# Layer 2 of a four-layer model: where the routing of its experts is issued, and how its streams are woven together

## The chip, the core and the metric

The kernel runs on one NeuronCore of a Trainium2 chip. Five engines work side by side, each through its own queue of instructions: TensorE (PE: matmuls and transposes, results to PSUM), VectorE (DVE), ScalarE (ACT), GpSimd (POOL) and SyncE (SP, which here only issues DMAs). The metric is the device time of one execution, in microseconds. The granted clock in the profile is TensorE's, as a share of full speed.

## The reference

Four layers work on 2048 tokens of width 256, four sequences of 512. Each layer takes the normalised tokens and adds a mixer and a feed-forward block. Only layer 2 and the end of layer 1 matter here. Layer 2:

```python
# mixer: 16 heads of 16; key and value are one head of 16
q = (x @ Wq.T + bq).reshape(b, l, h, hd)
kv = (x @ Wkv.T + bkv).reshape(b, l, 2, hd)
k, v = (kv[:, :, 0], kv[:, :, 1])
attn = softmax(einsum('blhd,bld->blh', q, k)[..., None] / sqrt(hd), axis=-1)
out = (attn * v[:, :, None, :]).reshape(b, l, -1)
# experts: the 2 best of 8 by a softmax router, and a shared expert of width 256
scores = softmax(einsum('th,eh->te', xf, gate_w), axis=-1)
topk_w, topk_i = top_k(scores, 2)
topk_w = topk_w / sum(topk_w, axis=-1, keepdims=True)
hgated = silu(einsum('th,ehi->eti', xf, wg)) * einsum('th,ehi->eti', xf, wu)
y = ...   # the two chosen experts' hgated @ wd, weighted by topk_w
shared = silu(xf @ sg) * (xf @ su) @ sd
```

The reference's softmax in the mixer is over an axis of length one, so that its weight is 1 whatever the score; the kernel computes it in full. Layer 1 is a latent attention with causal softmax beside product-key experts and a gated feed-forward block.

## The kernel before

The tokens lie in SBUF as 16 tiles of 128 (`c.x`), with their normalised transpose in `c.xnT`. A layer is a set of Python generators, its streams, each of which issues some instructions and then yields a cost. `weave` (L230 and on) always advances the stream whose progress, cost so far over its stated total, is least; a third number is the progress at which a stream joins. Thus the weave sets the order in which instructions are issued in the program. The framework's scheduler then fixes each engine's own order from the priority of issue, its own estimates of durations and the dependences, places the tiles and inserts the semaphores; where the text marks `keep_in_program_order`, an instruction may not be moved against its like. On the chip every engine's queue runs in the order so found, and an instruction that waits holds up all that stand behind it.

When all users of a sequence in a layer have added their part (`part_done`), the layer norm of that sequence is issued (L91 to L126): statistics and `xn` on DVE, a store of the rows to DRAM, and, some steps later or when `settle` asks for it, the transposes into `xnT`.

Layer 2 treats the tokens in two halves of 1024. A half's routing, `dispatch`, takes the router's matmuls for 8 tiles (L142 on `t_small`), a softmax on DVE and ACT, the rank of each of the 8 experts by comparison of all pairs, counts by three small matmuls (L1303), and from these a slot for every chosen token, such that each expert's tokens fill whole tiles: 23 tiles of 128 slots hold any outcome. To invert that (which token stands in slot s?), 16 masks `at` of 128x128 are made (L1353) and multiplied by `hit` (L1360), which yields `ids`. Then `gather` (L1396) fetches the tokens' rows by 23 indirect DMAs from POOL's queue; `experts` transposes them (L1414), multiplies by the slot tile's expert (L1426, at a column offset that PE reads from memory), applies SiLU (L1433, L1434), transposes again (L1440), multiplies (L1448), copies (L1453) and stores the result (L1455) to DRAM. `combine` later fetches for each token tile the two results by indirect DMAs (L1492) and adds them, weighted, to `c.x` (L152).

The shared expert is a `glu_pieces` (L134 up, L201, L202, L212 down, L158 adds to x). The mixer, `head_mix`, works sequence by sequence: projections (L142 on `h_small`) and bias (L1184), product with the key (L1189), sum (L1193), Exp (L1198), normalisation (L1199, L1200), then the product with the value on POOL (L1201) and the addition to x on DVE (L1206).

Layer 1's weave ends with `room`, which at progress 0.915 closes the pools of the product-key and feed-forward streams and opens layer 2's first tiles (`following.first()`), and does no more. Layer 2's `run` then has three weaves, one after another: the shared expert beside both halves' routing; the first half's experts beside the mixer and the second half's gathers; the second half's experts beside the first half's combine. The first half's gathers are issued pair by pair from within `experts`, three pairs of buffers ahead. The second half's combine runs inside layer 3.

## Time and profile before

| | us |
|---|---|
| runs shown: median (lowest, highest) | 3180.86 (3175.3, 3186.27) |
| the profiled execution | 3176.93 |
| its span, first to last instruction | 3175.2 |
| layer 1's last matmul for its output (L882) ends | 1537.4 |
| first `ids` (L1366) of half 0, half 1 | 1559.2, 1598.7 |
| first and last row gather (L1396) | 1560.1, 1651.5 |
| first and last expert matmul of L1426 | 1609.8, 1710.1 |
| POOL's four products (L1201) | 1632.9 to 1675.9 |

A line of the profile names the engine, the line of the code (of a helper, where one records the operation), the operation, the tile written and those read, and shapes. A line of the timeline gives the start, the time that a run of equal instructions took, their number, and in brackets how long the engine had stood idle and who ended it. A line of the groups gives the number, busy time and mean, and the idle time before them. A line of the stretches gives the length, then PE, its weight loads, DVE, ACT and POOL each with busy time and number of instructions, and last the granted clock, DMA share and GB/s. Each float32 matmul shows as two instructions. A line of the waits gives who waited for whom, the sum, the number of waits, and the longest.

### The profile page before, as it was taken

The page shows a single profiled execution, that of the slowest core. Times are in us where ns is not written, and L with a number is a line of the kernel's source. Part 1 is how long each engine was busy: PE and PEld are TensorE (multiplying, and loading weights), DVE is VectorE, ACT ScalarE, POOL GpSimd, SP SyncE. Part 2 cuts the span into 40 slices and gives each one's busy share as a digit, 9 for nine tenths or more (in the row PEclk, how much of TensorE's full clock was granted, in tenths as well). Part 3 has the DMA queues.
Part 4 walks back from the last instruction along what each step waited for, and adds up shares of the span by engine and source line. Part 5 has one row for each costly group of instructions (what it writes and reads, how often), then busy time and mean ns, then how long its engine had stood idle before and what let it go on. Part 6 is the DMA issues. An engine that isn't in the chain of part 4 may idle for free.

```text
span 3175.2 us, 35804 instructions
## 1 busy us (share of the span) xinstructions
PE 3091.7 (97%) x12502; PEld 1890.4 (60%) x12502; DVE 1847.0 (58%) x4714; ACT 1259.5 (40%) x2910; POOL 636.4 (20%) x525
## 2 busy tenths in 40 slices
PE   8999999999899999999889999999999999999999
PEld 5566566565655555555566566566666665555555
DVE  5878778787677787777546654554554522222222
ACT  4444444443356666667425433333333401111111
POOL 0464455555400132331153000000000000000000
PEclk9999999999899999999889999999999999999999
DMA  3233233332311244444143000000000000000000
GB/s 130 83 104 123 87 97 111 102 108 75 107 37 35 62 123 102 114 110 132 38 107 110 7 21 7 1 27 1 21 1 1 20 20 20 20 20 20 1 0 27
DMA packets 89092, 185.16 MB, mean 58 GB/s; under 512 B 14193, under 2 KB 57217, under 8 KB 84177
## 3 DMA queue, kind: packets, MB, share of 16 engines
q1 hardware_dynamic: 74448, 135.05, 13.2%
q0 software_dynamic: 14176, 47.01, 6.0%
q8 instruction: 99, 1.62, 0.2%
q10 hardware_dynamic: 288, 0.82, 0.1%
q14 instruction: 81, 0.66, 0.1%
HBM read 160.95 MB, written 12.98 MB: 55 GB/s over the span
## 4 chain that ended last, share of the span: by engine, by line
PE 80%; DVE 10%; DMA 4%; ACT 2%; POOL 2%; issue 1%; SPq 1%; DVEq 0%; ACTq 0%; POOLq 0%
PE mm L134 31%; PE acc L212 8%; PE mm L643 7%; PE mm L142 5%; PE acc L1115 4%; PE acc L659 3%; DMA G<-own 3%; PE tr L1107 2%; PE tr L507 2%; DVE G L421 2%; PE tr L824 2%; PE acc L868 2%; DVE cy L280 2%; PE acc L486 1%; PE tr L212 1%
## 5 line engine op out<-in xcount | busy, mean ns | idle before, releaser
L134 PE MATMUL mm<-xnT,wu 128*128 128x512 f32 x2128 | 960.3, 598 | 2.9 <-DVE cy L280 1.3
L134 PEld LDWEIGHTS mm<-xnT,wu 128*128 128x128 f32 x2128 | 400.4, 191 | 464.5 <-issue 434.9
L650 ACT ACTIVATE pr<-pr,nm 128x128 f32<-128x128 f32 (+3 forms) x512 | 285.9, 559 | 293.5 <-DVE nm L646 290.9
L201 ACT ACTIVATE sg<-mm 128x512 f32<-128x512 f32 x176 | 104.5, 594 | 611.2 <-PE mm L134 611.1
L202 DVE TENSOR_TENSOR hT<-sg,mm 128x512 f32<-128x512 f32 x176 | 120.5, 685 | 385.8 <-PE mm L134 369.8
L646 DVE CUSTOM_DVE_ANT_0 pr<-mm,late 128x128 f32<-128x128 f32 (+3 forms) x512 | 245.2, 482 | 85.2 <-PE mm L643 80.3
L212 PE MATMUL acc<-wu,hT 128*128 128x256 f32 x1280 | 289.5, 382 | 1.9 <-DVE hT L202 1.4
L212 PEld LDWEIGHTS acc<-wu,hT 128*128 128x128 f32 x1280 | 243.2, 191 | 53.1 <-issue 18.0
L134 PE MATMUL mm<-xnT,w_in 128*128 128x512 f32 x512 | 230.9, 597 | 0.0
L986 POOL DMA_INDIRECT e<-in_p_experts,ids x128 | 128.1, 1001 | 453.6 <-DVE x L152 413.3
L421 DVE TENSOR_TENSOR_SCAN G<-G,eye 128x1024 f32<-128x1024 f32 x64 | 158.3, 2474 | 66.9 <-DMA G<-own 66.8
L447 POOL TENSOR_TENSOR G<-G,CB 128x1024 f32<-128x1024 f32 x64 | 151.9, 2374 | 176.4 <-DVE G L421 97.1
L643 PE MATMUL mm<-kf,qf 128*128 128x128 f32 (+3 forms) x512 | 176.2, 443 | 6.5 <-DVE qf L801 4.1
L643 PE MATMUL mm<-k,q 128*128 128x128 f32 (+3 forms) x512 | 176.6, 435 | 1.1 <-DVE q L1080 1.1
L280 DVE SCALAR_TENSOR_TENSOR cy<-mm,ws,cy 128x511 f32<-128x511 f32 (+2 forms) x216 | 158.4, 741 | 32.6 <-ACT cy L276 29.2
L134 PEld LDWEIGHTS mm<-xnT,w_in 128*128 128x128 f32 x512 | 97.6, 192 | 103.4 <-issue 97.8
L433 ACT ACTIVATE xD<-xc,ws 128x128 f32<-128x128 f32 x256 | 84.2, 391 | 176.8 <-POOL y L470 162.0
L152 DVE SCALAR_TENSOR_TENSOR x<-acc,cw,x 128x256 f32<-128x256 f32 x128 | 62.0, 484 | 155.6 <-PE acc L212 155.6
L1115 PE MATMUL acc<-PT,V 128*128 128x512 f32 (+3 forms) x512 | 149.5, 433 | 0.0
L1080 DVE TENSOR_SCALAR q<-mm,bias 128x512 f32<-128x512 f32 x64 | 48.0, 751 | 169.0 <-PE mm L134 169.0
L824 PEld LDWEIGHTS tr<-con,pr 128*128 128x128 f32 x640 | 80.5, 142 | 95.6 <-ACT pr L817 30.5
L507 PE MATMUL tr<-wo,y 128*128 128x256 f32 x512 | 126.7, 391 | 7.9 <-DVE x L158 4.0
(309 smaller groups left out, 4948.3 us busy)
## 6 DMA issues: line engine op xcount, KB each, us to landing
G<-own SPq DMA_DIRECT2D x64, 512.0 KB, 4.3
w_in<-in_m_units SPq DMA_DIRECT2D x16, 1024.0 KB, 5.1
eb<-since SPq DMA_DIRECT2D x96, 128.0 KB, 3.4
wu<-in_o_units SPq DMA_DIRECT2D x8, 1536.0 KB, 6.5
wo<-in_m_units SPq DMA_DIRECT2D x16, 512.0 KB, 4.1
psw<-pes SPq DMA_DIRECT2D x128, 64.0 KB, 2.8
wu<-in_g_units SPq DMA_DIRECT2D x4, 1536.0 KB, 6.9
wu<-in_f_units SPq DMA_DIRECT2D x4, 1536.0 KB, 8.2
```

The source lines that it names most:

```text
L134: c.nc.tensor.matmul(out, lhsT=w[:, d, cols], rhs=c.xnT[:, d, tokens], start=(d == 0), stop=(d == 1))
L142: c.nc.tensor.matmul(out, lhsT=c.xnT[:, d, tokens], rhs=w[:, d, cols], start=(d == 0), stop=(d == 1))
L212: nc.tensor.matmul(po[:, j, :], lhsT=hT[k][:, (t + j) * P : (t + j + 1) * P], rhs=wd[:, k, :], start=(i == 0), stop=(i == per - 1),)
L280: nc.vector.scalar_tensor_tensor(y[:, j:], src[:, : SEQ - j], conv[:, k, 3 - j : 4 - j], y[:, j:], ALU.mult, ALU.add,)
L421: nc.vector.tensor_tensor_scan(flat, flat, eye.rearrange("p h t -> p (h t)"), 0.0, ALU.mult, ALU.add)
L447: nc.gpsimd.tensor_mul(G, G, seqs[b][2][:, t, :][:, None, :].to_broadcast([P, HG, P]))
L507: nc.tensor.matmul(po, lhsT=y[:, k, :], rhs=groups[i][1][:, k, :], start=(k == 0), stop=(k == 3))
L643: nc.tensor.matmul(sc, lhsT=q[:, i * P : n], rhs=k[:, :n], start=True, stop=True)
L646: nc.vector.tensor_tensor_reduce(out=pr, in0=sc, in1=late[:, SEQ - n :], scale=1.0, scalar=-NEG, op0=ALU.add, op1=ALU.min, accum_out=nm,)
L650: nc.scalar.activation(pr, pr, AF.Exp, bias=nm, scale=-1.0, accum_out=total)
L824: nc.tensor.transpose(pt[:, (i - j) * P : (i - j + 1) * P], prs[s][i][:, j * P : (j + 1) * P], c.ident)
L1115: nc.tensor.matmul(z[:, j * P :], lhsT=head["V"][:, j, h, :], rhs=head["PT"][:, j, j * P :], start=(j == 0), stop=(j == TPB - 1),)
```

## The change

`room` in layer 1 goes on with the first half's routing after opening the tiles, and is given a total of 270 in place of 1, so that its 21 units of cost take it from 0.915 to about 0.99 of the weave. The two first weaves of layer 2 become one: the shared expert, the first half's gathers (a stream of its own), the second half's routing followed by its gathers, the first half's experts, and the mixer. The third weave stays; the combine joins at 0.15 in place of 0.2. Gathered rows have one ring of 20 pair buffers in place of 3 and 12.

In the routing, a router call serves both sequences of a half at once; the running sum over 8 tiles takes three doubling steps in place of eight single ones; the tile number (`token`) is multiplied into `hit` once, and the 16 masks are made by four wide comparisons in place of sixteen narrow ones, in the ring of buffers (`before`, 4) that the router's comparisons use; all matmuls of L1360 follow the masks in one run. The mixer takes two sequences at a time, with one Exp for both, a yield after it, and the second product on DVE in place of POOL, which keeps only DMAs. Layer 3's router uses the same function with one sequence a call.

```diff
@@ -1043,13 +1043,14 @@
             right.close()
             following.first()
             yield 1.0
+            yield from following.routing(0)
 
         weave(
             c,
             (latent, 457.0, 0.0),
             (product_key_pieces(c, a, p_keep, p_t, dram, xn), 232.0, 0.0),
             (glu_units(), 145.0, 0.0),
-            (room(), 1.0, 0.915),
+            (room(), 270.0, 0.915),
             flush=False,
         )
 
@@ -1169,43 +1170,51 @@
 
 
 
-def head_mix(c, pool, w, b):
+def head_mix(c, pool, w, bs):
 
     nc = c.nc
     H, HD, W = 16, 16, 288
     wqkv = v3(w[:, : 2 * W], W)
     bias = w[:, 2 * W : 3 * W]
-    qkv = c.tile(pool, [P, TPB, W], "qkv")
-    c.settle(b)
-    for t in range(TPB):
-        tt = b * TPB + t
-        pq = c.ps()[:, :W]
-        project_tokens(c, pq, wqkv, slice(0, W), slice(tt * P, (tt + 1) * P))
-        nc.vector.tensor_add(qkv[:, t, :], pq, bias)
-        yield 0.5
+    n = len(bs) * TPB
     full = [P, TPB, H, HD]
-    prod = c.tile(pool, full, "prod")
     heads = lambda v: v.rearrange("p t (h d) -> p t h d", d=HD)
-    nc.vector.tensor_mul(
-        prod, heads(qkv[:, :, :256]), qkv[:, :, 256:272][:, :, None, :].to_broadcast(full)
-    )
-    s = c.tile(pool, [P, TPB, H], "s", bufs=2)
-    nc.vector.tensor_reduce(s, prod, AX.X, ALU.add)
-    top = c.tile(pool, [P, TPB, H], "top", bufs=2)
+    qkv = c.tile(pool, [P, n, W], "qkv")
+    s = c.tile(pool, [P, n, H], "s")
+    parts = [slice(i * TPB, (i + 1) * TPB) for i in range(len(bs))]
+    for b, part in zip(bs, parts):
+        c.settle(b)
+        for t in range(TPB):
+            tt = b * TPB + t
+            pq = c.ps()[:, :W]
+            project_tokens(c, pq, wqkv, slice(0, W), slice(tt * P, (tt + 1) * P))
+            nc.vector.tensor_add(qkv[:, part.start + t, :], pq, bias)
+            yield 0.5
+        prod = c.tile(pool, full, "prod")
+        nc.vector.tensor_mul(
+            prod, heads(qkv[:, part, :256]),
+            qkv[:, part, 256:272][:, :, None, :].to_broadcast(full),
+        )
+        nc.vector.tensor_reduce(s[:, part], prod, AX.X, ALU.add)
+    top = c.tile(pool, [P, n, H], "top")
     nc.vector.tensor_copy(top, s)
     nc.vector.tensor_sub(s, s, top)
     nc.scalar.activation(s, s, AF.Exp, scale=HD ** -0.5)
+    yield 1.0
     nc.vector.reciprocal(top, s)
     nc.vector.tensor_mul(s, s, top)
-    nc.gpsimd.tensor_mul(
-        prod, s[:, :, :, None].to_broadcast(full),
-        qkv[:, :, 272:288][:, :, None, :].to_broadcast(full),
-    )
-    x = c.x[:, b * TPB : (b + 1) * TPB, :]
-    nc.vector.tensor_add(x, x, prod.rearrange("p t h d -> p t (h d)"))
-    c.part_done(b)
-    yield 1.0
+    for b, part in zip(bs, parts):
+        prod = c.tile(pool, full, "prod")
+        nc.vector.tensor_mul(
+            prod, s[:, part, :, None].to_broadcast(full),
+            qkv[:, part, 272:288][:, :, None, :].to_broadcast(full),
+        )
+        x = c.x[:, b * TPB : (b + 1) * TPB, :]
+        nc.vector.tensor_add(x, x, prod.rearrange("p t h d -> p t (h d)"))
+        c.part_done(b)
+        yield 0.5
 
 
 def softmax(c, s, m, scale):
@@ -1220,28 +1229,31 @@
     nc.vector.tensor_mul(s, s, m[:, :, None].to_broadcast(wide))
 
 
-def router(c, pool, wr, b, p=None):
+def router(c, pool, wr, bs, p=None, wide=1):
 
 
     nc = c.nc
-    E = 8
-    c.settle(b)
-    pl = c.ps()[:, : TPB * E]
-    for t in range(TPB):
-        tt = b * TPB + t
-        project_tokens(
-            c, pl[:, t * E : (t + 1) * E], wr, slice(0, E), slice(tt * P, (tt + 1) * P)
-        )
-    yield 0.5
+    E, n = 8, len(bs) * TPB
+    pl = c.ps()[:, : n * E]
+    for i, b in enumerate(bs):
+        c.settle(b)
+        for t in range(TPB):
+            tt, to = b * TPB + t, (i * TPB + t) * E
+            project_tokens(
+                c, pl[:, to : to + E], wr, slice(0, E), slice(tt * P, (tt + 1) * P)
+            )
+    yield 2.0
     if p is None:
         p = c.tile(pool, [P, TPB, E], "p")
     nc.vector.tensor_copy(p, v3(pl, E))
-    m = c.tile(pool, [P, TPB], "m")
+    m = c.tile(pool, [P, n], "m")
     softmax(c, p, m, 1.0)
-    full = [P, TPB, E, E]
+    yield 2.0
+    full = [P, n, E, E]
     other, own = p[:, :, None, :].to_broadcast(full), p[:, :, :, None].to_broadcast(full)
-    before = c.tile(pool, full, "before")
-    tie = c.tile(pool, full, "tie")
+    before = c.tile(pool, full, "before", bufs=wide)
+    tie = c.tile(pool, full, "before" if wide > 1 else "tie", bufs=wide)
     nc.vector.tensor_tensor(before, other, own, ALU.is_gt)
     nc.vector.tensor_tensor(tie, other, own, ALU.is_equal)
     low = v3(c.low, E)[:, None, :, :].to_broadcast(full)
@@ -1274,30 +1286,34 @@
         c, k, pool, nc = self.c, self.k, self.pool, self.c.nc
         tile = lambda shape, tag, **kw: c.tile(pool, shape, tag, **kw)
         p, rank = tile([P, HT, E8], "p_half"), tile([P, HT, E8], "rank")
-        for i in range(2):
-            tiles = slice(i * TPB, (i + 1) * TPB)
-            before = yield from router(c, pool, k["router"], 2 * self.hf + i, p[:, tiles, :])
-            nc.vector.tensor_reduce(rank[:, tiles, :], before[2], AX.X, ALU.add)
-            yield 1.0
+        before = yield from router(c, pool, k["router"], [2 * self.hf, 2 * self.hf + 1], p, 4)
+        yield 2.0
+        nc.vector.tensor_reduce(rank, before[2], AX.X, ALU.add)
 
         both = [P, 2, HT, E8]
         sel = tile(both, "sel")
         for r in range(2):
             nc.vector.tensor_scalar(sel[:, r], rank, float(r), None, ALU.is_equal)
-        chosen = tile([P, HT, E8], "chosen")
+        Z = 4
+        cum = tile([P, 4, Z + HT, E8], "cum")
+        nc.vector.memset(cum[:, :, :Z, :], 0.0)
+        chosen = cum[:, 0, Z:, :]
         nc.vector.tensor_scalar(chosen, rank, 2.0, None, ALU.is_lt)
-        cum = tile([P, HT + 1, E8], "cum")
-        nc.vector.memset(cum[:, 0, :], 0.0)
-        for t in range(HT):
-            nc.vector.tensor_add(cum[:, t + 1, :], cum[:, t, :], chosen[:, t, :])
-        yield 1.0
+        for step in range(3):
+            last, back = cum[:, step], 1 << step
+            nc.vector.tensor_add(
+                cum[:, step + 1, Z:, :], last[:, Z:, :], last[:, Z - back : Z - back + HT, :]
+            )
+        before_tile, in_all = cum[:, 3, Z - 1 : Z - 1 + HT, :], cum[:, 3, Z + HT - 1, :]
+        yield 3.0
         flat = lambda v: v.rearrange("p t e -> p (t e)")
         pc = c.ps()
         n = HT * E8
         for out, lhsT, rhs, start, stop in (
             (pc[:, :n], c.le, flat(chosen), True, False),
-            (pc[:, :n], c.ones, flat(cum[:, :HT, :]), False, True),
-            (pc[:, n : n + E8], c.ones, cum[:, HT, :], True, True),
+            (pc[:, :n], c.ones, flat(before_tile), False, True),
+            (pc[:, n : n + E8], c.ones, in_all, True, True),
         ):
             c.tc.keep_in_program_order(
                 nc.tensor.matmul(out, lhsT=lhsT, rhs=rhs, start=start, stop=stop)
@@ -1344,25 +1360,29 @@
             k["iota"][:, :NS][:, None, :].to_broadcast(by_tile), ALU.is_equal,
         )
         nc.vector.scalar_tensor_tensor(part, part, -float(P), slot, ALU.mult, ALU.add)
+        split = hit.rearrange("p (r t) j -> p r t j", r=2)
+        nc.vector.tensor_mul(
+            split, split, k["token"][:, None, :, None].to_broadcast([P, 2, HT, NS])
+        )
         yield 1.0
         ats = []
-        for i in range(2 * HT + 4):
-            if i < 2 * HT:
-                ats.append(tile([P, P], "at", bufs=8))
-                t = i % HT
-                nc.vector.tensor_scalar(
-                    ats[i], k["iota"], part[:, i : i + 1], k["token"][:, t : t + 1],
-                    ALU.is_equal, ALU.mult,
-                )
-            if i == 4:
-                pid = c.ps()[:, :NS]
-            if i >= 4:
-                c.tc.keep_in_program_order(nc.tensor.matmul(
-                    pid, lhsT=ats[i - 4], rhs=hit[:, i - 4, :], start=(i == 4),
-                    stop=(i == 2 * HT + 3),
-                ))
-            if i % 4 == 3:
-                yield 1.0
+        four = [P, 4, P]
+        for i in range(2 * HT // 4):
+            ats.append(tile(four, "before", bufs=4))
+            nc.vector.tensor_tensor(
+                ats[i], k["iota"][:, None, :].to_broadcast(four),
+                part[:, 4 * i : 4 * i + 4][:, :, None].to_broadcast(four), ALU.is_equal,
+            )
+            yield 1.0
+        yield 1.0
+        pid = c.ps()[:, :NS]
+        for m in range(2 * HT):
+            c.tc.keep_in_program_order(nc.tensor.matmul(
+                pid, lhsT=ats[m // 4][:, m % 4, :], rhs=hit[:, m, :], start=(m == 0),
+                stop=(m == 2 * HT - 1),
+            ))
+        yield 1.0
         nc.vector.tensor_copy(self.ids, pid)
         one = [1, NS, E8]
         done = tile([P, NS, E8], "done")
...
 
-    def gather(self, pool, bufs, js):
-        for j in js:
-            x = self.xs[j] = self.c.tile(pool, [P, 2, DM], f"xs{self.hf}", bufs=bufs)
-            for i, t in enumerate(PAIRS[j]):
-                self.c.nc.gpsimd.indirect_dma_start(
+    def gather(self, pool):
+        for j, pair in enumerate(PAIRS):
+            x = self.xs[j] = self.c.tile(pool, [P, 2, DM], "xs", bufs=20)
+            for i, t in enumerate(pair):
+                self.c.tc.keep_in_program_order(self.c.nc.gpsimd.indirect_dma_start(
                     out=x[:, i, :], out_offset=None, in_=self.xn,
                     in_offset=bass.IndirectOffsetOnAxis(ap=self.ids[:, t : t + 1], axis=0),
-                )
+                ))
             yield 1.0
...
@@ -1537,27 +1552,26 @@
             h_small = c.tile(mixer, [P, 864], "h_small")
             c.nc.sync.dma_start(h_small, a["h_unit"])
 
-            def dispatch():
-                for half in self.halves:
-                    yield from half.dispatch()
+            first, last = self.halves
 
             def mix():
-                for b in range(NB):
-                    yield from head_mix(c, mixer, h_small, b)
+                for hf in range(2):
+                    yield from head_mix(c, mixer, h_small, [2 * hf, 2 * hf + 1])
+            def second():
+                yield from self.routing(1)
+                yield from last.gather(xs)
 
             shared = glu_pieces(c, mixer, [unit], n=2, width=256, loaded=True, bufs=4)
-            first, last = self.halves
-            every = range(len(PAIRS))
-            experts = [
-                half.experts(self.weights, temp, self.rows, more)
-                for half, more in ((first, first.gather(xs, 3, every)), (last, None))
-            ]
-            weave(c, (shared, 41.0, 0.0), (dispatch(), 34.0, 0.0), flush=False)
+            experts = [half.experts(self.weights, temp, self.rows) for half in self.halves]
             weave(
-                c, (experts[0], 40.0, 0.0), (mix(), 12.0, 0.0),
-                (last.gather(xs, len(PAIRS), every), 12.0, 0.0), flush=False,
+                c, (shared, 44.0, 0.0), (first.gather(xs), 24.0, 0.0), (second(), 38.0, 0.08),
+                (experts[0], 45.0, 0.1), (mix(), 15.0, 0.0), flush=False,
             )
-            weave(c, (experts[1], 40.0, 0.0), (first.combine(self.rows), 11.0, 0.2), flush=False)
+            weave(c, (experts[1], 40.0, 0.0), (first.combine(self.rows), 11.0, 0.15), flush=False)
+    def routing(self, hf):
+        return self.halves[hf].dispatch()
 
     def rest(self):
         yield from self.halves[1].combine(self.rows)
```

## The prediction

> **What bounds the kernel now.** I read the page first. TensorE (PE) is busy 97% of the span and carries 80% of the chain that ended last, so time is gained only where PE stands still or runs slowly. The 40 slices of the page show one such place: the granted clock and the busy digits dip in slices 18 to 20, about 1430 to 1670 us. By the timeline that is layer 1's tail and layer 2. Layer 1's last matmul for its output ends at 1537.4, the first half's experts end at 1672, the second half's at 1714. So I asked for the busy time of every engine in these three stretches and in the worst 14 us.
>
> ```profile
> span 3175.2 us, 35804 instructions
> PE 3091.7 (97%) x12502; PEld 1890.4 (60%) x12502; DVE 1847.0 (58%) x4714; ACT 1259.5 (40%) x2910; POOL 636.4 (20%) x525
> ...
> core 0: us, PE busy (x) PEld busy (x) DVE busy (x) ACT busy (x) POOL busy (x), PEclk, DMA share, GB/s
> 1472.00:1537.00 65.00, 60.73 (x293) 36.21 (x292) 41.61 (x149) 46.66 (x119) 1.16 (x2) 0.97 0.30 101
> 1537.00:1672.00 135.00, 118.83 (x507) 87.85 (x506) 73.42 (x212) 38.89 (x65) 52.80 (x49) 0.89 0.30 82
> 1672.00:1714.00 42.00, 40.34 (x217) 33.90 (x216) 27.81 (x68) 23.39 (x46) 18.66 (x17) 1.00 0.42 128
> ...
> 1629.00:1643.00 14.00, 6.87 (x21) 5.14 (x20) 4.36 (x9) 0.91 (x3) 7.77 (x7) 0.63 0.35 88
> ```
>
> To see: the middle stretch has only 118.83 us of PE in 135, at a mean clock of 0.89; the last one is nearly full at clock 1.00. Then I listed the PE groups of the middle stretch by shape, to price it at full clock.
>
> ```profile
> L134 PE MATMUL mm<-xnT,wu 128*128 128x512 f32 x50 | 29.4, 724 | 0.0
> L1426 PE MATMUL mm<-weights,xsT 128*128 x92 | 23.9, 404 | 7.1 <-DVE qkv L1184 7.1
> L142 PE MATMUL mm<-h_small,xnT 128*128 128x288 f32 x64 | 19.1, 423 | 0.0
> L212 PE MATMUL acc<-wu,hT 128*128 128x256 f32 x64 | 18.2, 436 | 1.6 <-DVE hT L202 1.4
> L1360 PE MATMUL mm<-hit,at 128*128 128x23 f32 x64 | 9.3, 285 | 3.0 <-DVE at L1353 3.0
> ```
>
> The last stretch and layer 3 give rates at full clock: 3.45 us for eight 512-wide matmuls (0.431 each), 1.73 for eight 256-wide (0.216), 0.97 for four 288-wide (0.243), 0.87 for eight transposes (0.108); the 8- and 23-wide ones take about 0.106. The stretch is then 21.6 (L134) + 19.9 (L1426) + 15.5 (mixer) + 13.8 (L212) + 9.9 (46 at L1448) + 6.8 (L1360) + 3.4 (32 router matmuls) + 7.9 (73 transposes of rows and hidden) + 0.9 + 1.3 + 0.4 (layer norm, counts, layer 1's rest) = 101.4 us of work. So 33.6 of the 135 us are lost, to waits and to a low clock. The timeline shows both.
>
> ```profile
> 1522.20 3.71 PE L142 MATMUL mm<-t_small,xnT 128*128 128x8 f32 x32
> 1525.91 1.61 PE L134 MATMUL mm<-xnT,wu 128*128 128x512 f32 x2
> ...
> 1629.06 0.38 PE L1440 MATMUL tr<-con,hs 128*128 128x128 f32 x2
> 1636.57 3.75 PE L1426 MATMUL mm<-weights,xsT 128*128 x8 [7.13 <-DVE qkv L1184]
> 1640.11 2.12 PE L142 MATMUL mm<-h_small,xnT 128*128 128x288 f32 x4
> ```
>
> After 3.7 us of eight-wide matmuls two 512-wide ones take 1.61 where 1.02 is usual in this view; after a 7.13 us wait eight 256-wide ones take 3.75 for 1.89. Who made PE wait those 7.13 us stands in VectorE's (DVE) and GpSimd's (POOL) timelines and in the list of waits:
>
> ```profile
> 1631.89 0.94 POOL L1396 DMA_INDIRECT xs<-xn_half,ids  x1 [0.30 <-issue]
> 1632.85 1.94 POOL L1201 TENSOR_TENSOR prod<-s,qkv 128x1024 f32<-128x1024 f32 x1
> ...
> 1634.83 1.23 DVE L1206 TENSOR_TENSOR x<-x,prod 128x1024 f32<-128x1024 f32 x1 [10.92 <-POOL prod L1201]
> ...
> DVE x L1206 <- POOL prod L1201: 15.9, 4, 10.9
> ...
> POOL xs L1396 <- DVE ids L1366: 96.2, 2, 86.1
> ```
>
> The mixer's second product stood on POOL behind a run of row gathers (one each 1.25 us since 1599); DVE stood behind the product, PE behind DVE. Before that POOL had no ids until 1560: routing comes late, and the experts, which hold 37 us of good PE work per half, can't start before 1609.
>
> [...] here the product took 1.93 us on POOL, and DVE products of this shape 1.23. [...] most gathers here took 0.95 us and a few up to 1.96, so I price that at nothing.
>
> **The change, part by part.**
>
> *First half routed in layer 1's tail.* About 7.4 us of PE work per half (3.4 router, 0.6 counts, 3.4 for L1360's half) goes into 1472 to 1537. In the profile that tail already holds the first router (3.7) and 14 matmuls of the shared GLU; the newcomers are 4.0 us, and the tail has 4.3 us of PE idle. On DVE one half's routing is about 16 us: one router for 8 tiles (five passes over 128x512 by 0.69 = 3.5, softmax 1.2), 1.3 for selection and the three-step running sum (eight adds of 0.16 before), 2.1 counts and slots, 2.6 for the hits with the new multiply, four wide masks by 0.69 = 2.8 (sixteen of 0.27 in sequence before), 2.3 for the rest. Some 6 of it was in the tail, so DVE goes from 41.6 to about 52 of 65 us, ACT (46.7) gains almost nothing and has Exp loaded. This fills neither queue, but the attention's chain passes DVE. The trace doesn't show how much of the 10 us lies in that chain: between -2 (PE gaps filled better) and +10 (all of it). I take +2, since DVE still idles a fifth; of PE's 4.0 I take half as hidden in its idle time, +2.
>
> *Gather.* Twenty-three gathers by 1.25 = 29 us of POOL. The rows' pool lies where layer 1's tiles were (ACT's first shared activation waited for L882 until 1537.45), so they start at about 1540 instead of 1560 and never stop for a buffer (19.7 us of waits before, with three). First rows at about 1540 + 2.5 + 3.5 to land = 1546; the experts start at a tenth of the weave, some 10 us of PE work, 6 of which still run ahead inside the tail. I allow 2 us of waiting. The second half's ids come at 0.6 of the weave, about 1600; its 29 us of gathers end near 1630, before its experts at about 1650: hidden.
>
> *One weave.* Its PE work is 101.4 minus the half routing of 4.0, about 97. DVE gets the product (4 by 1.23 = 4.9) and loses the first routing (about 11): 67 us, so PE stays the bound. The mixer in pairs keeps its work and has two Exps instead of four; with the second routing's one Exp that is six table loads of 1.28 beside Silu, on an ACT busy under half. The 7.1 us wait and its cold 3 us go; so do most of the gaps around 1538 to 1600, since the experts' matmuls fill them. What stays: two bursts of narrow matmuls in the weave, each followed by a cold window, about 2 us each and 4 in all; start-up behind layer 1's end with two table loads, 3; the rows, 2; head-of-line waits among DVE's users, PSUM buffers and table loads, 5 (between 0 and 15, from nothing to half of DVE's idle 62 us that might turn to waits). Loss about 14 instead of 33.6.
>
> *Second half.* The same 42 us; the first half's combine (16 gathers by 1.25 = 20 us on POOL) starts a little earlier and stays hidden; 39.5 us of work, nothing to win.
>
> **Sum.** Layer 1's tail +4; weave 97 + 14 = 111 for 135, that is -24; second half 0. Together -20 us. The profiled execution took 3176.93 (span 3175.2): 3156.9. The median of the runs shown, 3180.86, lies 0.12% above it, which would make 3160.9. I say 3158.
>
> **Rivals.**
> *Nearly all of it* (chance 0.22): the weave loses 6 us as the second half does (2 of 42), and the tail absorbs routing: 97 + 6 = 103, -32, about 3146. For it: the second half's stage and 1643 to 1672 run at clock 1.00. Against it: neither has narrow bursts or routing in it.
> *Given back in the tail* (0.16): routing lies in the attention's chain: +10 on DVE and +4 on PE, and 3 of cold clock from narrow bursts in the tail; -24 becomes about -7, 3170. For it: DVE and ACT are already busy 64% and 72% there. Against it: the scheduler put half a router in already, at little cost.
> *Slower: DVE's queue in one weave* (0.12). Five users (GLU, experts, mixer, routing, layer norm) share one DVE order with runs of 1.2 us operations and waits on ACT's table loads; if an entry waits, all PSUM buffers behind it stay full, PE stops, goes cold, and the next entries wait in turn. With 67 us of DVE work it decides from about 68 us of DVE waits, that is if today's 62 all stay and layer 1's tail loses 10: 67 + 62 + 10 + 4 = 143 for 135, +8 to +15, about 3190. Against it: 62 us today are mostly waits for work that doesn't exist yet.
> That routing doesn't move forward at all, since its tiles find no room beside layer 1's, is within these last two.
>
> **How the numbers follow.** Chances: forecast 0.50, nearly all 0.22, given back 0.16, slower 0.12. A measurement of this kernel tells about 0.3%, 9.5 us, from no change. Faster: 0.50 + 0.22 + a third of 0.16 = 0.77; slower 0.11; between 0.12. The range takes the nearly-all case to its full 3142 and the given-back case to 3178: 3142 to 3178. The forecast's own range is 3150 to 3167.
>
> **What would show it.** Right: first gather near 1540, first expert matmul before 1560, no PE wait on the mixer over 2 us, no product on POOL, mean clock in the weave above 0.95, the stretch from layer 1's end to the second half near 111 us. Wrong: layer 1's end later than 1545; PE waits on DVE spread over the weave; rows that arrive after their transposes.

## The result, and a second result for the same kernel

The kernel after took 3160.91 us (median of 6), the kernel before beside it 3187.59 (6): ratio 0.9924, interval 0.9905 to 0.9944. The forecast was 3158. The same kernel, run again in a later job on chip 4, took 3217.50 us (12) beside 3203.33 for the kernel before (39): ratio 1.0042, interval 1.0029 to 1.0055. The ratios and their 95% intervals are those on record; they need not equal the quotient of the two medians. The first part of what follows reads the first result, the rest is the search for what lies between the two.

The page of the kernel after, its first profile:

```profile
span 3154.9 us, 35717 instructions
PE 3082.5 (98%) x12502; PEld 1885.9 (60%) x12502; DVE 1841.9 (58%) x4656; ACT 1249.8 (40%) x2898; POOL 627.9 (20%) x521
```

The three stretches again, cut where layer 1's last output matmul and the first half's experts now end (columns as in the prediction):

```profile
1476.00:1547.50 71.50, 65.88 (x328) 40.29 (x327) 47.70 (x172) 50.48 (x121) 1.16 (x2) 0.98 0.29 98
1547.50:1651.00 103.50, 103.09 (x473) 78.64 (x472) 66.50 (x139) 30.68 (x56) 44.98 (x46) 0.97 0.36 93
1651.00:1693.60 42.60, 40.26 (x214) 33.39 (x213) 25.76 (x66) 20.20 (x42) 15.63 (x16) 1.00 0.47 151
```

The middle stretch fell from 135.0 us with 118.83 of PE at clock 0.89 to 103.5 with 103.09 at 0.97: PE no longer stands still in it. PE's waits for other engines between 1547 and 1652, all of them (total, times, longest):

```profile
PE acc L1468 <- ACT hsT L1462: 0.4, 1, 0.4
```

Layer 1's end moved from 1537.4 to 1547.5. Of these 10.1 us, 4.5 come from before any changed instruction (the run of L868 that starts at 1462.86 before starts at 1467.39 after; the first instruction that was moved, the router's first matmul, starts at 1485.0) and 5.6 from the tail itself. So the profiled spans differ by 20.3 us, and the changed stretch gained about 25: +5.6 in the tail, -31.5 in the weave, +0.6 in the second half.

How the first half's rows, the second router and the mixer now share PE is seen at the weave's start, in the timeline of the kernel after (start, duration, engine, line):

```profile
1557.20 0.95 POOL L1416 DMA_INDIRECT xs<-xn_half,ids  x1 [0.30 <-issue]
...
1558.10 0.79 PE L1434 MATMUL tr<-con,xs 128*128 128x128 f32 x4
1558.28 0.23 DVE L1249 COPY p_half<-mm 128x64 f32<-128x64 f32 x1 [2.71 <-PE mm L142]
...
1558.68 2.13 PE L142 MATMUL mm<-h_small,xnT 128*128 128x288 f32 x4
...
1558.97 0.59 ACT L1439 COPY xsT<-tr 128x512 f32<-128x512 f32 x1 [4.38 <-PE tr L1434]
...
1560.60 0.63 PE L1446 MATMUL mm<-weights,xsT 128*128 x1
```

The last router matmul starts at 1557.99 in the trace; DVE reads its PSUM 0.29 us later. The four mixer matmuls at 1558.68 take 2.13 us instead of 1.13: one of the weave's two cold windows (stretches of half clock in the trace's record of it), here behind the 32 narrow matmuls of the router (3.63 us from 1554.61). The mean granted clock is 0.50 from 1558.5 to 1561.8 and from 1609.7 to 1613.0, and 1.00 from 1562 to 1609. While all that runs, GpSimd (POOL) issues 23 gathers in a row, 1548.4 to 1577.2.

### The profile page after: what moved, and what is told of

It is laid out like the page before. It is cut to its first block, busy times and chain, and to the rows that moved or that the text cites. A ratio compares the mean times of both kernels' runs of the same rounds, so it can differ in the third digit from the quotient of the medians.

```text
span 3154.9 us, 35717 instructions
## 1 busy us (share of the span) xinstructions
PE 3082.5 (98%) x12502; PEld 1885.9 (60%) x12502; DVE 1841.9 (58%) x4656; ACT 1249.8 (40%) x2898; POOL 627.9 (20%) x521
## 2 busy tenths in 40 slices
DMA packets 89090, 185.15 MB, mean 59 GB/s; under 512 B 14192, under 2 KB 57216, under 8 KB 84176
## 4 chain that ended last, share of the span: by engine, by line
PE 79%; DVE 11%; DMA 5%; ACT 2%; POOL 2%; issue 2%; SPq 1%; DVEq 0%; ACTq 0%; POOLq 0%
PE mm L134 30%; PE acc L212 9%; PE mm L643 7%; PE mm L142 5%; PE acc L1116 4%; PE acc L659 4%; DMA G<-own 3%; DVE G L421 2%; PE tr L1108 2%; DVE cy L280 2%; PE tr L824 2%; PE tr L507 2%; PE acc L868 2%; PE mm L1446 1%; PE tr L212 1%
## 5 line engine op out<-in xcount | busy, mean ns | idle before, releaser
L986 POOL DMA_INDIRECT e<-in_p_experts,ids x128 | 128.4, 1003 | 454.1 <-DVE x L152 413.4
```

## The experiments

Twelve kernels ran, in four jobs; a job keeps to one chip, and each kernel's ratio is to the kernel before on that chip in that job.

| job, chip | kernel | median us (runs) | ratio | interval |
|---|---|---|---|---|
| 1, chip 4 | e1 after, product on GpSimd | 3203.18 (20) | 1.0005 | 0.9997 to 1.0013 |
| 1 | e2 after, first routing in the weave | 3213.43 (11) | 1.0045 | 1.0033 to 1.0058 |
| 1 | e3 after, two weaves | 3223.26 (5) | 1.0067 | 1.0045 to 1.0088 |
| 1 | e4 before, product on VectorE | 3199.96 (12) | 0.9997 | 0.9981 to 1.0013 |
| 2, chip 4 | c1 after, unaltered | 3217.50 (12) | 1.0042 | 1.0029 to 1.0055 |
| 2 | e5 before, first routing in the tail | 3195.65 (12) | 0.9982 | 0.9966 to 0.9997 |
| 2 | e6 after, narrow burst split | 3211.38 (15) | 1.0026 | 1.0014 to 1.0038 |
| 2 | e7 after, narrow masks | 3216.91 (7) | 1.0042 | 1.0024 to 1.0060 |
| 3, chip 0 | e8 after, gathers paced | 3169.29 (20) | 0.9955 | 0.9942 to 0.9968 |
| 3 | e9 before, second half's gathers paced | 3181.49 (20) | 0.9994 | 0.9979 to 1.0008 |
| 3 | e10 after, rows by plain transfers | 3158.70 (6) | 0.9915 | 0.9885 to 0.9946 |
| 4, chip 15 | e11 after, first half's gathers paced | 3200.84 (14) | 0.9982 | 0.9971 to 0.9994 |

The kernel before took 3200.08, 3203.33, 3183.93 and 3207.29 us in the four jobs. Which chip the first comparison ran on isn't recorded.

### Parts of the change: e1 to e4

e1, on the kernel after (L1210):

```diff
-        nc.vector.tensor_mul(
+        nc.gpsimd.tensor_mul(
```

> The changed kernel with one part undone: the mixer's second product is on GpSimd again. Theory A (the product must not stand in the queue of the row gathers): the product of one pair falls behind 23 gathers of 1.25 us or behind their wait for ids, the vector engine waits for it by 5 to 25 us at a time, TensorE follows, and layer 2's stretch from layer 1's end to the second half's experts grows from 103.5 to 110 or more; 7 us or more are lost of the 24 gained. Theory B (with the gathers early the queue is empty when the product comes, and the move to the vector engine is incidental): within 3 us of the changed kernel, about 0.9925 of the kernel before.

e2, on the kernel after:

```diff
-            yield from following.routing(0)
...
-            (room(), 270.0, 0.915),
+            (room(), 1.0, 0.915),
...
+            def opening():
+                yield from quick(self.routing(0))
+                yield from first.gather(xs)
+            def quick(g):
+                for _ in g:
+                    yield 0.3
...
-                c, (shared, 44.0, 0.0), (first.gather(xs), 24.0, 0.0), (second(), 38.0, 0.08),
-                (experts[0], 45.0, 0.1), (mix(), 15.0, 0.0), flush=False,
+                c, (shared, 44.0, 0.0), (opening(), 30.0, 0.0), (second(), 38.0, 0.08),
+                (experts[0], 45.0, 0.3), (mix(), 15.0, 0.0), flush=False,
```

> The changed kernel, but the first half's routing is issued at the head of the one weave in place of layer 1's tail (its experts join at 0.3 in place of 0.1). Theory A (early routing is what lets the weave fill): layer 1's tail shortens by 4 to 6 us, first ids come about 20 us after its end, and the weave grows by 12 to 20 us, since the narrow matmuls and the gathers' start have only the shared expert and the mixer beside them; net 7 to 14 us slower than the changed kernel (0.995 to 0.997 of the kernel before). Theory B (one weave alone does it; shared expert and mixer, 57 us of matmuls, cover the routing): the weave grows by no more than the 7 us of routing matmuls, the tail gives 5 back, within 3 us of the changed kernel.

e3, on the kernel after:

```diff
-                c, (shared, 44.0, 0.0), (first.gather(xs), 24.0, 0.0), (second(), 38.0, 0.08),
-                (experts[0], 45.0, 0.1), (mix(), 15.0, 0.0), flush=False,
+                c, (shared, 44.0, 0.0), (first.gather(xs), 24.0, 0.0), (self.routing(1), 24.0, 0.08),
+                flush=False,
+            )
+            weave(
+                c, (experts[0], 45.0, 0.0), (mix(), 15.0, 0.0), (last.gather(xs), 12.0, 0.0),
+                flush=False,
```

> The changed kernel with the one weave split as before: shared expert, first gathers and second routing first; then the first half's experts, the mixer and the second gathers. Routing in layer 1's tail, wide masks, pairs in the mixer and the product on the vector engine stay. Theory A (merging is what fills the gaps): the first of the two stretches loses again to narrow bursts, table loads and waits behind the shared expert, some 10 to 15 us; 0.996 of the kernel before. Theory B (early routing and the free GpSimd queue are enough): within 4 us of the changed kernel, 0.993.

e4, on the kernel before (L1201): the same edit as e1, in the other direction.

> The kernel before with one part of the change alone: the mixer's second product on the vector engine. Theory A: the 7.1 us wait of TensorE at the first product and the cold 3 us behind it go, the second half's gathers lose their last interruptions; 8 to 11 us faster, 0.997 of the kernel before. Theory B (the wait is only taken over by another, the gathered rows or PSUM): within 4 us of the kernel before.

All three altered versions of the kernel after came out no faster than the kernel before, which would have given every part of the change more than the whole of its gain. That was hard to believe, and the traces gave a reason to doubt the measure: each had several stretches, the longest of 9.9 to 14.0 us, in which PE, DVE and ACT all stood still ("stops" from here on, if 1 us or longer), some of them before the first altered instruction, in layer 1. e4 can be read against the kernel before, but only for this chip: the product on VectorE brings nothing there (theory B). Its trace has stops of 8.0 and 2.1 us in the mixer's stretch (1626.8 to 1640.4), where the profile of the kernel before has PE's wait for the product, so what the product is worth without stops isn't shown. The control, the kernel after on this chip, was missing.

### The control: c1

The kernel after, without any edit, in one job with e5 to e7.

> The kernel after the change, not altered, as the measure for the runs beside it and for the first batch, whose kernels showed stalls of 10 to 20 us in which all engines stood still and which the profile of the kernel after does not have. Theory A (the gain is real and those stalls came with the altered kernels): ratio to before 0.991 to 0.995, no stall over 5 us on TensorE between 1500 and 1700. Theory C (the stalls belong to the chip or the session, and would take part of the gain of any version): ratio 0.998 to 1.005, with such stalls in this trace too.

Theory C held: 1.0042, and the stops are in this trace too. Against c1, not against 0.9924, must e1 to e3 be read: e2 takes as long as c1 (1.0045), e3 some 8 us more (0.25%), and e1, which puts the product back on GpSimd, is 12 us faster (1.0005 against 1.0042). Their expectations were set around 0.9925, so none of their ranges fits. Part of the differences lies in the stops: between 1440 and 1800 us they add up to 39.2 us in c1, 22.5 in e1, 28.7 in e2 and 23.6 in e3. As an estimate from these sums, which takes a stop to cost its own length, the three would be about 5, 11 and 24 us slower than c1 if none had stops. That is the side of theory A in all three, but it is not a measurement.

The first stop, in c1's timeline at the same instructions as above:

```profile
1564.00 3.63 PE L142 MATMUL mm<-t_small,xnT 128*128 128x8 f32 x32
...
1567.49 0.83 PE L1434 MATMUL tr<-con,xs 128*128 128x128 f32 x4
1567.85 0.95 POOL L1416 DMA_INDIRECT xs<-xn_half,ids  x1 [0.30 <-issue]
...
1585.37 0.94 POOL L1416 DMA_INDIRECT xs<-xn_half,ids  x1 [0.30 <-issue]
1590.16 0.22 DVE L1249 COPY p_half<-mm 128x64 f32<-128x64 f32 x1 [25.21 <-remote]
1590.27 0.59 ACT L1439 COPY xsT<-tr 128x512 f32<-128x512 f32 x1 [26.29 <-remote]
...
1590.90 3.78 PE L1446 MATMUL mm<-weights,xsT 128*128 x8 [20.66 <-ACT xsT L1439]
```

The router's last matmul starts at 1567.38, and DVE reads it at 1590.16: 22.8 us instead of 0.29. ACT's copy of the transposes starts within 0.11 us of it. The trace has no update of PE's semaphore between 1561.55 and 1590.14, then three within 0.12 us. Eight are due in that stretch. Five of them (1562.65 to 1564.16) have no record at all, though ACT acted in time on what they tell: its copy L126 starts at 1562.90, at the same place as in the first profile. The last three, of matmuls that end at 1567.63, 1568.33 and 1570.24 by the trace, are the ones recorded at 1590.14 to 1590.26. So some records were lost, and then PE's results came up to 22.5 us late, all at once. Whether the matmuls or only their announcement was late can't be told: the ends of matmuls are modelled in the trace.

In all of c1's trace, 56 updates of PE are recorded more than 0.3 us after the latest end of one of its updating matmuls, the end of the program apart, and none of DVE or ACT after theirs; in the first profile there is none of either kind. DVE and ACT stand still because they wait for PE, and PE in turn for ACT. "remote" is the profile's word for a releaser that it did not find. Of the computing engines only GpSimd goes on during the stop, and the stop ends 3.9 us after the last of the 23 gathers.

c1's weave and second half follow. From here on the cuts are layer 1's end, the second half's first expert matmul and layer 3's first query (1547.5, 1652.0 and 1703.9 in the first profile, so 104.5 and 51.9 us there):

```profile
1556.90:1700.90 144.00, 108.85 (x479) 80.96 (x477) 66.66 (x140) 31.14 (x58) 43.63 (x46) 0.86 0.26 69
1700.90:1760.40 59.50, 51.27 (x239) 39.16 (x239) 26.67 (x66) 24.59 (x50) 16.34 (x17) 0.94 0.39 125
```

Of the 60.6 us between the two spans of one and the same kernel, 39.5 are in the weave (31.1 of them its stops), 7.6 in the second half, 7.5 in layer 1's attention (first L868 to last L882: 629.9 for 622.4), the rest outside.

In e1 the product stands in GpSimd's queue between the gathers and breaks their run, as its timeline (POOL alone) shows:

```profile
1578.01 0.94 POOL L1416 DMA_INDIRECT xs<-xn_half,ids  x1 [0.30 <-issue]
1609.46 1.93 POOL L1210 TENSOR_TENSOR prod<-s,qkv 128x1024 f32<-128x1024 f32 x1 [30.50 <-DVE s L1207]
```

The product waits 30.50 us for DVE, and the five gathers that stand behind it and the next one start only at 1616.52. The first run has 18 gathers instead of 23, 1556.6 to 1579.0; the first stop is 14.0 us instead of 19.9. Five gathers less are 6.25 us less of GpSimd at 1.25 each, and the stop is 5.9 shorter; no later one is over 2 us. This fits e1's lead over c1: on this chip the arrangement that the change removed is the better one.

### Routing in the tail alone, narrow bursts, masks: e5 to e7

e5, on the kernel before:

```diff
             following.first()
             yield 1.0
+            yield from following.halves[0].dispatch()
...
-            (room(), 1.0, 0.915),
+            (room(), 240.0, 0.915),
...
-                for half in self.halves:
-                    yield from half.dispatch()
+                yield from self.halves[1].dispatch()
...
-            weave(c, (shared, 41.0, 0.0), (dispatch(), 34.0, 0.0), flush=False)
+            weave(c, (shared, 41.0, 0.0), (dispatch(), 17.0, 0.0), flush=False)
```

> The kernel before with one part of the change alone: the first half's routing, in its old form, is issued in layer 1's tail; the rest of layer 2 stays in its weaves and the mixer stays in one stream with its products on GpSimd. Theory A (most of the loss stood in the stretch in which TensorE had nothing but routing and shared expert, and the routing in the tail removes part of it alone): layer 1 ends 4 to 6 us later, the time to the second half falls by 12 to 20 us, sum 8 to 16 us faster than before, ratio 0.995 to 0.9975. Theory B (only the one weave gains; the routing moved alone is given back): ratio 0.999 to 1.003.

0.9982 lies between the two ranges: 5.8 us gained where 8 to 16 were asked. Layer 1's attention takes 632.7 us (e4, on the same chip and with the tail of the kernel before: 624.8), the time from layer 1's end to the second half 121.1 (e4: 140.7). So the part works by itself, and about 8 of some 20 us are given back in the tail. Its trace has stops of 2.7 and 7.7 us in a run of 23 gathers.

e6, on the kernel after (L1381's loop):

```diff
                 stop=(m == 2 * HT - 1),
             ))
-        yield 1.0
+            if m % 4 == 3:
+                yield 1.0
```

> The kernel after with the 32 narrow matmuls of the position of each token issued four tiles (8 matmuls) at a time, other streams in between. Theory A (a burst of 3.6 us of narrow matmuls is what lowers the clock, 1.6 to 1.9 us of loss behind each): in the trace the wide matmuls behind the narrow ones keep their usual duration (L142 at 1.13 us, not 2.1 to 2.2) and the weave from layer 1's end to the second half is 2 to 4 us shorter; time 2 to 4 us below the unaltered one. Theory B (the clock falls for another reason): the slow matmuls stay, time within 2 us of the unaltered one.

In c1's timeline (PE alone) the burst and what follows it:

```profile
1540.65 3.90 PE L1381 MATMUL mm<-hit,before 128*128 128x23 f32 x32
1544.37 3.41 PE L134 MATMUL mm<-xnT,wu 128*128 128x512 f32 x4
```

and in e6's:

```profile
1542.37 0.97 PE L1381 MATMUL mm<-hit,before 128*128 128x23 f32 x8
1543.18 2.82 PE L134 MATMUL mm<-xnT,wu 128*128 128x512 f32 x6
```

Four 512-wide matmuls took 3.41 us behind 32 narrow ones, six took 2.82 behind eight, which is near the usual rate (1.88 for four), and the half-clock window of 3.4 us at 1544 is gone from e6's record of the clock. So here half clock follows the burst of 32 matmuls of 23 columns, though PE is busy all through it (3.90 us), as the prediction took it, and not the eight at 1542.37 (0.97 us). Not every such burst is followed by it. Behind c1's second one four mixer matmuls take 1.22 us, near the usual 1.13, and the record shows full clock from 1595.1 to 1663.4:

```profile
1637.92 3.65 PE L1381 MATMUL mm<-hit,before 128*128 128x23 f32 x32
1641.41 1.22 PE L142 MATMUL mm<-h_small,xnT 128*128 128x288 f32 x4
```

In the first profile the same burst, at 1606.09, was followed by half clock (0.50 from 1609.7 to 1613.0; the four mixer matmuls took 2.21 us); what decides isn't shown. e6's time is 6.1 us below c1's, with intervals that overlap (1.0014 to 1.0038, 1.0029 to 1.0055), and its stops add up to 33.9 us instead of 39.2, which alone would account for most of that. So theory A holds for the clock behind the burst that was split; the price in the whole isn't shown.

e7, on the kernel after:

```diff
-            nc.vector.tensor_tensor(
-                ats[i], k["iota"][:, None, :].to_broadcast(four),
-                part[:, 4 * i : 4 * i + 4][:, :, None].to_broadcast(four), ALU.is_equal,
-            )
+            for j in range(4):
+                nc.vector.tensor_scalar(
+                    ats[i][:, j, :], k["iota"], part[:, 4 * i + j : 4 * i + j + 1], None, ALU.is_equal
+                )
```

> The kernel after with the masks made by sixteen comparisons of one tile for each of four of four tiles, as before the change; the values are the same. Theory A (the wide masks were a small saving on VectorE, none of the gain hangs on them): VectorE 1 to 3 us more for each half, time within 3 us of the unaltered one. Theory B (VectorE is the bound in layer 1's tail, so that every microsecond there counts): layer 1's end 1.5 to 4 us later, time 3 to 6 us slower.

1.0042, as c1; theory A. The first stops of e6 and e7 (19.0 and 19.7 us) are c1's within 1 us, so neither the burst of L1381 nor the masks make it.

### Gathers in a row: e8 to e11

e8, on the kernel after:

```diff
-            x = self.xs[j] = self.c.tile(pool, [P, 2, DM], "xs", bufs=20)
+            x = self.xs[j] = self.c.tile(pool, [P, 2, DM], f"xs{self.hf}", bufs=4)
...
             if j + 1 < N:
                 turn(j + 1)
+                next(more, None)
...
-                yield from last.gather(xs)
+                yield from last.gather(xs, range(4))
...
-            experts = [half.experts(self.weights, temp, self.rows) for half in self.halves]
+            experts = [
+                half.experts(self.weights, temp, self.rows, half.gather(xs, range(4, len(PAIRS))))
+                for half in self.halves
+            ]
...
-                c, (shared, 44.0, 0.0), (first.gather(xs), 24.0, 0.0), (second(), 38.0, 0.08),
+                c, (shared, 44.0, 0.0), (first.gather(xs, range(4)), 60.0, 0.0), (second(), 30.0, 0.08),
```

> The kernel after with the row gathers paced: four pairs of tiles ahead in a ring of four, then one pair for each step of the experts, so that GpSimd never issues more than eight in a row there. In the unaltered kernel's second profile the semaphore updates of TensorE's work of 1567 to 1570 arrive at 1590, some 4 us after the last of 23 gathers in a row; in its first profile the same run of gathers delays nothing. Theory D (a long run of gathers holds back the semaphores of all engines in these runs, and the change lengthened the runs): no stop of all engines over 4 us between 1540 and 1720, the weave from layer 1's end to the second half 103 to 115 us instead of some 140, time 20 to 40 us below the unaltered kernel, ratio to before 0.990 to 0.997. Theory E (the stops come from the router's narrow matmuls or from TensorE's register loads): stops as before, ratio 1.002 to 1.006.

e9, on the kernel before:

```diff
-                for half, more in ((first, first.gather(xs, 3, every)), (last, None))
+                for half, more in (
+                    (first, first.gather(xs, 3, every)),
+                    (last, chain([0, 0], last.gather(xs, 3, range(2, len(PAIRS))))),
+                )
...
-                (last.gather(xs, len(PAIRS), every), 12.0, 0.0), flush=False,
+                (last.gather(xs, 3, range(2)), 3.0, 0.75), flush=False,
```

> The kernel before with the second half's gathers paced like those of its first half (two pairs ahead, then one for each step, in a ring of three). Theory D: the stop of 8 to 10 us near 1615 to 1635 that the two altered versions of the kernel before showed is gone or below 3 us, time 8 to 16 us less, ratio 0.995 to 0.9975; what is then left between this and the paced kernel after is the change's own gain, 10 to 25 us. Theory E: ratio 0.999 to 1.001. A loss of 2 to 6 us in the second half is possible for either, where rows arrive late behind the combine's gathers.

e10, on the kernel after:

```diff
-                self.c.tc.keep_in_program_order(self.c.nc.gpsimd.indirect_dma_start(
-                    out=x[:, i, :], out_offset=None, in_=self.xn,
-                    in_offset=bass.IndirectOffsetOnAxis(ap=self.ids[:, t : t + 1], axis=0),
-                ))
+                at = t % HT * P
+                self.c.nc.sync.dma_start(x[:, i, :], self.xn[at : at + P, :])
```

> The kernel after with the experts' rows read by plain transfers from the sync queue, tile by tile in the order of the tokens, instead of gathers by GpSimd; the rows are therefore not those that the router chose, all else is left. Theory D with the fault in the gathers as GpSimd issues them: no stop over 4 us in the weave, ratio 0.988 to 0.995. Theory F (any dense traffic of small rows does it, whoever issues it): stops of the same size. Theory E: stops of the same size, since the router and the register loads are unaltered.

This job ran on chip 0, and none of its traces has a stop of this kind, not even where 31 (e8) or 28 gathers (e9) stand in a row (e9's one pause of 1.3 us is a wait for rows). So the three could not tell D from E, which is what they were for. What they give is the price of pacing where there are no stops. The unaltered kernel after did not run in this job; e10 and the first profile stand for it. e10's weave and second half:

```profile
1551.70:1656.20 104.50, 103.86 (x478) 79.30 (x476) 66.80 (x140) 31.34 (x58) 0.00 (x0) 0.97 0.31 95
1656.20:1707.90 51.70, 49.52 (x239) 38.08 (x239) 26.62 (x66) 24.74 (x50) 16.40 (x17) 1.00 0.46 145
```

104.5 and 51.7 us, with no gather of the experts' rows on GpSimd, are the 104.5 and 51.9 of the kernel after's first profile: there the gathers cost nothing, as the prediction had it. e8's:

```profile
1555.80:1661.60 105.80, 102.45 (x477) 78.31 (x477) 67.31 (x137) 34.55 (x61) 33.88 (x31) 0.98 0.28 79
1661.60:1722.90 61.30, 51.38 (x239) 37.88 (x239) 26.55 (x66) 24.94 (x50) 30.57 (x32) 1.00 0.51 156
```

and, of PE's waits in it (1655 to 1725):

```profile
PE tr L1435 <- DMA xs<-xn_half,ids: 5.7, 6, 1.9
```

Pacing the first half is nearly free (105.8), pacing the second costs 9.4 us; 5.7 of it are waits for rows, which queue on GpSimd among the rows of combine. e11 keeps the free half. It is e8's edit with the second half's gathers left as they were:

```diff
-                yield from last.gather(xs)
+                yield from last.gather(xs, len(PAIRS), every)
...
+                first.experts(self.weights, temp, self.rows, first.gather(xs, 4, every[4:])),
+                last.experts(self.weights, temp, self.rows, iter(())),
...
-                c, (shared, 44.0, 0.0), (first.gather(xs), 24.0, 0.0), (second(), 38.0, 0.08),
+                c, (shared, 44.0, 0.0), (first.gather(xs, 4, every[:4]), 60.0, 0.0), (second(), 38.0, 0.08),
```

> The kernel after with the gathers of the first half alone paced (four pairs ahead in a ring of four, then one pair for each step of its experts); the second half's are issued in one go, as in the kernel after. It separates the two halves of the paced kernel, whose second half took 61 us instead of 52 to layer 3's first query. On a chip that shows no stops: theory G (that loss is the second half's rows, queued on GpSimd behind the rows of combine, and pacing the first half costs nothing): weave from layer 1's end 102 to 107 us, second half 51 to 54 us, ratio to before 0.990 to 0.995; theory H (any pacing costs): ratio 0.995 to 0.999. On a chip that shows the stops: theory D: the first stop of 20 us is gone or below 5 us, the second of 7 us behind the second half's 23 gathers stays, ratio 0.995 to 0.999; theory E: both stay, ratio 1.002 to 1.006.

This time the chip, number 15, was one with stops. e11's weave and second half:

```profile
1563.70:1685.40 121.70, 105.46 (x477) 78.98 (x476) 66.80 (x140) 31.09 (x58) 47.09 (x46) 0.93 0.31 82
1685.40:1746.40 61.00, 53.08 (x239) 40.23 (x239) 26.82 (x67) 24.66 (x50) 16.31 (x17) 0.94 0.39 123
```

GpSimd's waits in it say what paces the gathers now, PE's transposes:

```profile
POOL xs L1417 <- PE tr L1435: 17.1, 5, 5.6
```

There is no stop at its first eight gathers nor at the paced ones. A short delay of the same kind is left behind the eight: DVE reads the router's result, due at 1574.43, at 1576.12, and three updates of PE are recorded within 0.11 us from 1576.10 on, 1.8 us after the last gather of the eight.

```profile
1573.39 0.94 POOL L1417 DMA_INDIRECT xs<-xn_half,ids  x1 [0.30 <-issue]
...
1576.12 0.22 DVE L1249 COPY p_half<-mm 128x64 f32<-128x64 f32 x1 [4.36 <-PE mm L142]
```

There are stops of 1.6 and 10.2 us at the second half's 24, and the second ends 3.3 us after the last of them:

```profile
1654.71 0.95 POOL L1417 DMA_INDIRECT xs<-xn_half,ids  x1 [0.30 <-issue]
1658.98 0.69 DVE L158 TENSOR_TENSOR x<-acc,x 128x512 f32<-128x512 f32 x1 [14.71 <-issue]
1659.76 0.37 ACT L1463 COPY hsT<-tr 128x256 f32<-128x256 f32 x1 [19.80 <-remote]
...
1660.19 2.08 PE L1469 MATMUL acc<-weights,hsT 128*128 x4 [11.38 <-ACT hsT L1463]
```

That is theory D: router, register loads, narrow bursts and mixer stand where they stood in c1, only the run of gathers is cut, and the first stop is gone. The weave takes 121.7 us for c1's 144.0, and the ratio is 0.9982, within D's 0.995 to 0.999. c1 ran on chip 4 and not on 15, so the 0.6% between them is not one comparison; the stop that is gone and the stop that stayed are in one trace. Theories G and H were left untried.

Runs of gathers after 1440 us that bear on this, from the start and duration of every instruction:

| kernel | gathers in a row | issued | stops, us | the last stop ends, us after the last gather |
|---|---|---|---|---|
| c1, layer 1 (L986) | 8 | 1452.6 to 1462.9 | 3.2 | 1.1 |
| c1, first half | 23 | 1557.8 to 1586.3 | 19.9 | 3.9 |
| c1, second half | 23 | 1642.1 to 1670.5 | 1.4, 2.2, 7.5 | 3.9 |
| c1, combine | 10 | 1706.7 to 1719.0 | 4.9 | 1.9 |
| e1, first half | 18 | 1556.6 to 1579.0 | 14.0 | 3.2 |
| e2, first half | 23 | 1577.2 to 1607.1 | 8.2, 1.5 | 2.8 |
| e2, second half | 23 | 1632.6 to 1661.0 | 13.0 | 1.0 |
| e3, first half | 23 | 1566.4 to 1595.1 | 4.8 | 3.2 before it |
| e3, second half | 22 | 1630.3 to 1657.6 | 9.9, 1.6 | 3.7 |
| e6, first half | 23 | 1557.3 to 1585.9 | 19.0 | 3.8 |
| e7, first half | 23 | 1556.4 to 1584.9 | 19.7 | 3.9 |
| e4 (before), second half | 23 | 1608.3 to 1636.8 | 8.0, 2.1 | 3.6 |
| e5 (before), second half | 23 | 1593.6 to 1622.1 | 2.7, 7.7 | 1.7 |
| e11, layer 1 (L986) | 8 | 1458.3 to 1468.4 | 3.3 | 1.3 |
| e11, first half | 8 | 1564.5 to 1574.3 | none | |
| e11, second half | 24 | 1626.0 to 1655.7 | 1.6, 10.2 | 3.3 |
| after, first profile, first half | 23 | 1548.4 to 1577.2 | none | |
| e8, second half and combine | 31 | 1667.4 to 1706.2 | none | |

The number of gathers alone doesn't set the stop: 23 in a row gave from 4.8 us (e3) to 19.9 (c1), and eight gave 3.3 us in e11's layer 1 and none in its first half. The kernel before has one long run, its second half's (in its versions e4 and e5: 23 gathers, 10.1 and 10.4 us of stops; no trace of the unaltered kernel before was kept from a chip with stops), and paces the first half's with three buffers. The change removed that pacing and so made a second long run, just where the experts start. c1's stop of 19.9 us stands in that run, and with the run cut, in e11, it is gone.

### What stays open

Whether the gathers as GpSimd issues them cause the stops, or any dense traffic of small rows (theory F): e10, which was to tell, ran where there are none. Why only PE's updates come late. And why the traces of some jobs have stops and those of others none, and whether that belongs to the chip or to the job. One thing goes with it without exception: the traces with stops have lost records. The records of semaphore updates by DMA number 10,987 to 10,992 in the first two profiles and in e8, e9 and e10 (chip 0), and 8,603 to 8,905 in the eight of chip 4 and in e11 (chip 15), while packets and instructions are as many (89,090 and 35,717 in the kernel after's page and in c1's). Of the updates by PE, ACT and DVE c1 lacks 342 of 8,780. The losses begin in layer 1's gathers. What is missing are records of semaphore updates, and the stops lie in the stretch of time that has the losses. That the stops are the price of recording in those jobs, and not of the kernel, is a guess from this coincidence alone and isn't shown: no run here was made without recording, and if the updates themselves were late in those jobs and records went missing as a consequence, the trace could look the same.

## Why the prediction was right, and what it missed

By its own steps, against the first result.

- *What bounds the kernel:* 33.6 us lost in the middle stretch. Held: the stretch became 31.5 us shorter.
- *Layer 1's tail, +4:* 5.6. PE's busy time in the tail rose by about 5 us (60.73 to 65.88) and its idle time from 4.3 to 5.6, so none of the new work went into the idle time, on which the prediction counted for 2. DVE's work rose by 6 (41.61 to 47.70), not by 10. The sign "layer 1's end later than 1545" came up (1547.5), but 4.5 us of that lie before the change.
- *Gather, from about 1540, rows at 1546, 2 us of waiting:* first gather at 1548.4, first expert matmul at 1560.6 ("before 1560" missed by less than 1 us), PE waited 0.4 us in all. The second half's were to end near 1630 and ended at 1639.8: hidden.
- *One weave, 97 + 14 = 111:* 103.5 for 135.0. The work was nearly right (103.09 us at a mean clock of 0.97 are about 100 at full clock, an estimate); the term that was mis-sized is the loss of 14, which came to 6.5. Start-up 3, rows 2 and head-of-line waits 5 all came to nearly nothing: PE is busy 103.09 of 103.5 us, so what is lost is nearly all low clock: two windows, 1.8 and 1.9 us beyond the usual durations, the "about 2 us each" that was taken. The rival "nearly all of it" had this weave (103).
- *Second half, 0:* +0.6.
- *Sum, -20:* the spans differ by 20.3, but as -31.5 in the weave against +5.6, +0.6 and 4.5 from before the change. That the total agrees so well, and with it the median (3160.91 for 3158), is luck: a weave 7.5 us better than forecast met 6.7 us of losses that were not in the sum.
- *Removed wait:* the prediction laid PE's 7.13 us to the product behind the gathers on GpSimd (in the kernel before the mean granted clock was 0.50 from 1632 to 1642, in and behind that wait). In the kernel after the wait is gone. e4, which takes only the product away, gained nothing (0.9997), but on a chip with stops and with stops in that very place. What the product's move carried of the gain is therefore open; the traces show only that PE now has work all through the weave.

What it missed is in the sentence that 23 gathers are "29 us of POOL" and "hidden". The rows' way was priced as time of one engine's queue and as landing time. On two of the chips PE, DVE and ACT stood still in long runs of gathers (up to 19.9 us at a time in c1 on chip 4, 10.2 in e11 on chip 15), and the step that was counted as a gain, "never stop for a buffer", is the one that made the run long. None of the rivals had that mechanism; the slower one was about DVE's queue, which never filled: DVE did 66.50 us of work in the weave, as priced (67), and PE waited for it nowhere.

## What to carry to other kernels

A buffer ring too short to let a queue run ahead may be doing a service: before widening it, ask what the unbroken run does to the rest of the core. Gathers a few pairs ahead of their user, paced by a small ring, cost 1.3 us in the first half here (a weave of 105.8 us for 104.5, one profile each) and removed the stop of 20 us where there was one; gathers paced behind another user of the same queue cost 9.4. And when every altered kernel comes out worse than the one that it alters, run the unaltered one beside them first.

## What the runs showed of the hardware that was not expected

- On two chips, updates of PE's semaphore in a run of row gathers were recorded up to 22.5 us late, several at once, and the engines that waited for them started only then; DVE's and ACT's own were not late (c1). The last stop of a run ended 1.0 to 3.9 us after its last gather in all runs of the table but one (e3). On another chip, runs of 28 and 31 did nothing of the kind.
- The same kernel's medians were 3160.91 and 3217.50 us, 1.8% apart, and the kernel before's 3183.93 to 3207.29: the sign of a change of 1% can depend on the chip or the job that it is measured in.
- The first stop of c1, 1570.2 to 1590.2, lies in a window of half clock from 1567.8 to 1595.1 (27.3 us), and the eight expert matmuls behind it took 3.78 us instead of 1.89: with them this stop cost some 1.9 us more than its own length, an estimate from these two durations.
- A burst of 32 matmuls of 23 columns (3.65 us) is followed by half clock in the first profile (1606.09; 0.50 from 1609.7 to 1613.0) and by full clock in c1 (1637.92; full from 1595.1 to 1663.4).
